# Weight preparation between the turns of attention in a four-layer transformer kernel

## Chip, cores and metric

The kernel runs on one core of a Trainium2 chip, as one program in fp32. The metric is device time in microseconds (us) of one execution; lower is better. Engines are named as in the profile: PE is the matmul engine (PEld its weight loads), DVE the vector engine, ACT the scalar engine, POOL the general one; SP issues most DMAs.

## What is computed

Four layers, each of them a half-weighted feed-forward, an attention and the same feed-forward again, on 1024 tokens (4 sequences of 256) of width 256, every block on the layer-normed x and added to x:

```
x = x + 0.5 * ffn0(norm(x));  x = x + attn0(norm(x));  x = x + 0.5 * ffn0(norm(x))
x = x + 0.5 * ffn1(norm(x));  x = x + attn1(norm(x));  x = x + 0.5 * ffn1(norm(x))
... the same for layers 2 and 3
```

What the change touches:

- attn0: 16 heads of 16. The scores are q.k to the power 4, causal, divided by their sum; no exponential.
- ffn0: silu(gate) * up, 688 hidden units. ffn1: 8 experts of 176 hidden units, the best 2 per token by a router, and a shared part of 352.
- attn1 works with a latent of 64 numbers per token, in the reference like this:

```
lat = rmsnorm(x @ wkv_a_w.T, norm_w);  k, v = split(lat @ wkv_b_w.T)
q = x @ wq_w.T + wq_b                    (16 heads of 128, half of each rotated by `freqs`)
o = softmax(mask(q k^T * scale)) v;      out = o @ out_w.T + out_b
```

  The rotation turns q and k of one head alike, so the kernel needs only the squared length of each pair of `freqs`, and it multiplies the weights of a head with each other: wq with the key half of wkv_b gives w.m (query weights that act on the latent directly), the value half of wkv_b with out_w gives w.n. This is "the merge".
- layer 2 needs its router, its shared expert's gate, up and down weights, and the taps and biases of three short convolutions, all transposed on PE before use ("the turns").

## The kernel before

**Tokens and order.** x lies in eight tiles of 128 tokens. `norm` (L164) takes the statistics per half (four tiles), a chain of small DVE instructions for the inverse root (`rsqrt`, L154), the normalized tile (L179), two PE transposes per tile (L135) and a copy into xT (by `copy`, L137, which alternates DVE and ACT). Every matmul goes through `mm` (L131), every addition to x through `add_to_x` (L203), so these lines stand for many groups in the profile; the tile names tell them apart: `mmb`, `trb` and `accb` are PSUM banks, `slot` a block of weights.

**Banks.** PSUM has eight banks. `banks(mm, tr, acc)` (L103) deals them out per stage. The feed-forwards have 4 for matmuls, 2 for transposes, 2 for sums. The two attentions have 0, 2, 2 and take the other four as two tiles of two banks each, named `s`, for scores (pool `l0s` in layer 0, `l1s` in layer 1).

**Layer-0 attention** (`l0_attn`, L339). Two kinds of generators: `tokens` makes q, k and v of 128 tokens, rotates and normalizes them and transposes them; `group` does four heads of one sequence: scores into two `s` tiles (16 rows per head), two squarings on ACT (L420, L421), the causal cut on POOL (L423), the sums over values into `accb` (L437, L439). The fourth group of a sequence also forms the denominators (L452), divides (L458) and multiplies by w.o. `staggered` (L473) drives them: in each turn every live generator makes one step, and one new generator may join, up to eight. There are 33 turns.

**Layer-1 attention** (`l1_attn`, L700) has 32 units (4 sequences by 8 pairs of heads) in the same manner, six at a time (L790): scores into an `s` tile, exponential on ACT (L755), division on POOL (L761), transposes through `trb`, context sums, and in the last unit of a sequence the multiplication by w.n.

**The merge** (`l1_attn_weights`, L606) is a generator of five steps. The first issues loads. The second does the prologue (squared lengths, two small transposes and those of w.a) and part 0, the others parts 1 to 3. Each part does four heads: `dk` on POOL (L665), eight transposes of out_w through `trb` with copies to `oT`, 16 matmul instructions into `mp`, 8 into `np_`, copies of both banks into the weight slot, 8 tiny matmuls for the bias, and it issues the next loads (`load`, L627, and `load_out`, L639; the buffer of `wo` is single). `mp` and `np_` (L668, L669) are two matmul banks.

**The turns.** `l2_ffn_weights` (L815) loads into a staging pool, transposes and copies: router, gate, up, down. The staging tile `b` of gate and up is single, so that up's load waits until gate has been transposed. `l2_attn_weights` (L1027) loads small tensors and transposes 15 blocks of 16 columns into one bank.

**Where they stand** (`program`, L1706): the first step of the merge before the first layer-0 feed-forward; parts 0 and 1 after layer-0 attention, before the second layer-0 feed-forward; parts 2 and 3 and both of layer 2's preparations after it, before the first layer-1 feed-forward.

The source order sets priorities only. The framework gives each engine a fixed order in which an instruction goes ahead of earlier ones when its operands and buffers are free sooner: the multiplication of L1041, which belongs to layer 2, runs at 69.42 us. The prologue and the first transposes of part 0 run from 248.54 on, in the attention's tail.

Of the kernel before, what the change touches and what calls it, by code (L numbers as in the profile page):

```python
# [2 lines left out]

# [6 lines left out]
F32 = mybir.dt.float32  # L10
# [8 lines left out]
P = 128  # L19
B, S, D = 4, 256, 256  # L20
# [202 lines left out]
def staggered(parts, width, apart):  # L223
    for _ in turns(parts, width, apart):
        pass
# [110 lines left out]
                m.add_to_x(t, o[:, :D], 0.5)  # L336


def l0_attn(m, w):  # L339

# [3 lines left out]
    nc, io = m.nc, m.io  # L344
    m.norm()
    with ExitStack() as ctx:
        pool = lambda name, bufs, **kw: ctx.enter_context(m.tc.tile_pool(name=name, bufs=bufs, **kw))
        one, wk, pairs = pool("l0a1", 1), pool("l0a", 2), pool("l0s", 2, space=PSUM)
# [116 lines left out]
        def parts():  # L465
            yield from (tokens(0, 0), tokens(0, 1))
            for b in range(B):
                for g in range(4):
                    yield group(b, g)
                    if b + 1 < B and g < 2:  # L470
                        yield tokens(b + 1, g)

        staggered(parts(), width=8, apart=1)  # L473

# [131 lines left out]
def l1_attn_weights(m, stage):  # L606
# [3 lines left out]
    nc, io = m.nc, m.io  # L610
# [35 lines left out]
    def trace():  # L646
        loads, o = [load(0), load(1)], load_out(0)
        yield
        nc.gpsimd.memset(len2[:, :64], scale)
        nc.vector.tensor_tensor(fr, fr, fr, ALU.mult)  # L650
        both = len2[:, 64:].rearrange("h (j r) -> h j r", r=2)
        for r in range(2):
            nc.vector.tensor_tensor(both[:, :, r], fr[:, :, 0], fr[:, :, 1], ALU.add)
        nc.vector.tensor_scalar(len2[:, 64:], len2[:, 64:], scale, None, ALU.mult)
        tb = m.tr_bank()
        m.tr(tb[:, :16], len2)
        m.tr(tb[:, 16:32], bq)
        for k in range(KC):
            m.tr(tb[:, 32 + k * 64 : 96 + k * 64], a[:, k * P : (k + 1) * P])
        nc.vector.tensor_copy(cols, tb[:, :32].rearrange("p (i h) -> p i h", i=2))  # L660
        nc.vector.tensor_copy(w.a, tb[:, 32:160].rearrange("p (k c) -> p k c", k=2))
        for g in range(4):
            q, kv = loads[g]
            dk = stage.tile([P, 4, 64], F32, name="dk", bufs=1)
            nc.gpsimd.tensor_tensor(  # L665
                dk, kv[:, 0], cols[:, 0, 4 * g : 4 * g + 4].unsqueeze(2).to_broadcast([P, 4, 64]), ALU.mult
            )
            mp = m.mm_bank().rearrange("p (k f) -> p k f", k=2)  # L668
            np_ = m.mm_bank().rearrange("p (f d) -> p f d", f=2)  # L669
            for i in range(4):  # L670
                if i % 2 == 0:
                    tb = m.tr_bank()
                    for j in range(2):
                        for k in range(KC):
                            m.tr(tb[:, (2 * j + k) * P : (2 * j + k + 1) * P], o[:, k, (i + j) * P : (i + j + 1) * P])
                    oT = stage.tile([P, 2, D], F32, name="oT", bufs=1)
                    m.copy(oT, tb.rearrange("p (j d) -> p j d", j=2))
                    for k in range(KC):
                        for j in range(2):
                            c = (i + j) * 64  # L680
                            m.mm(mp[:, k, c : c + 64], [(q[:, i + j, k * P : (k + 1) * P], dk[:, i + j, :])])
                    for j in range(2):
                        m.mm(np_[64 * j : 64 * j + 64, i // 2, :], [(kv[:, 1, i + j, :], oT[:, j, :])])
            m.copy(w.m[:, :, 256 * g : 256 * g + 256], mp)
            m.copy(w.n[:, 2 * g : 2 * g + 2, :], np_)
            bp = m.tr_bank()
            for i in range(4):
                out = bp[64 * (i % 2) : 64 * (i % 2) + 64, i // 2 : i // 2 + 1]
                m.mm(out, [(dk[:, i, :], cols[:, 1, 4 * g + i : 4 * g + i + 1])])
            nc.vector.tensor_copy(w.bg[:, 2 * g : 2 * g + 2], bp[:, :2])  # L690
            if g < 3:
                o = load_out(g + 1)
            if g < 2:
                loads.append(load(g + 2))
            yield
# [1 line left out]
    return w, trace()  # L697


def l1_attn(m, w):  # L700

    nc = m.nc
    m.norm()
    with ExitStack() as ctx:
# [82 lines left out]
                    m.mm(o[:, :D], [(ctxT[b][:, f, i * P : (i + 1) * P], w.n[:, f, :]) for f in range(8)])  # L787
                    m.add_to_x(2 * b + i, o[:, :D], 1.0)

        staggered((unit(b, p) for b in range(B) for p in range(8)), width=6, apart=1)  # L790

# [20 lines left out]
    return got  # L812


def l2_ffn_weights(m):  # L815
    nc, io = m.nc, m.io
    w = SimpleNamespace()
    w.r = m.small.tile([P, KC, 64], F32, name="l2_router")
    w.sg = m.small.tile([P, KC, 192], F32, name="l2_sg")
    w.su = m.small.tile([P, KC, 192], F32, name="l2_su")  # L820
    w.sd = m.small.tile([96, 2, D], F32, name="l2_sd")
    with m.tc.tile_pool(name="l2w", bufs=1) as wk:
        a = wk.tile([64, D], F32, name="a")
        nc.sync.dma_start(out=a, in_=io.L2_ffn_gate_w)
        tb = m.tr_bank()
        for k in range(KC):
            m.tr(tb[:, k * 64 : k * 64 + 64], a[:, k * P : (k + 1) * P])
        m.copy(w.r, tb[:, :128].rearrange("p (k e) -> p k e", k=KC))
        for src, out in ((io.L2_ffn_shared_gate_w, w.sg), (io.L2_ffn_shared_up_w, w.su)):
            a = wk.tile([96, 2, D], F32, name="b")  # L830
            nc.sync.dma_start(out=a, in_=src.rearrange("(f p) d -> p f d", p=96))
# [5 lines left out]
        a = wk.tile([P, 2, 192], F32, name="c")  # L837
        nc.sync.dma_start(out=a, in_=io.L2_ffn_shared_down_w.rearrange("(c p) f -> p c f", p=P))
        tb = m.tr_bank()
        for f in range(2):  # L840
            for c in range(2):
                m.tr(tb[:96, f * D + c * P : f * D + (c + 1) * P], a[:, c, f * 96 : f * 96 + 96])
        m.copy(w.sd, tb[:96, : 2 * D].rearrange("p (f d) -> p f d", f=2))
    return w


def l2_ffn(m, w, tables, tail=None):
# [176 lines left out]
                m.add_to_x(t, got[:, k], 0.5)  # L1024


def l2_attn_weights(m):  # L1027
# [15 lines left out]
    with m.tc.tile_pool(name="l2aw", bufs=1) as wk:  # L1043
        tb = m.tr_bank()
        for i, n in enumerate("qkv"):
            taps = wk.tile([16, P, 4], F32, name=f"taps{i}")
            nc.sync.dma_start(out=taps, in_=getattr(io, f"L2_attn_{n}cw").rearrange("(h p) j -> h p j", h=16))
            bias = wk.tile([16, P], F32, name=f"bias{i}")
            nc.sync.dma_start(out=bias, in_=getattr(io, f"L2_attn_{n}cb").rearrange("(h p) -> h p", h=16))
            for j in range(5):  # L1050
                at = (i * 5 + j) * 16
                m.tr(tb[:, at : at + 16], taps[:, :, j] if j < 4 else bias)
        m.copy(w.conv, tb[:, :240].rearrange("p (i j h) -> p i j h", i=3, j=5))
    return w


def l2_attn(m, w):
# [648 lines left out]
def program(tc, io):  # L1706
    with ExitStack() as ctx:
# [4 lines left out]
        with tc.tile_pool(name="small2", bufs=1) as small2:  # L1712
            with slots() as m.wts:
                with tc.tile_pool(name="small1", bufs=1) as m.small:
                    with tc.tile_pool(name="l1w", bufs=2) as stage:
# [73 lines left out]
```

## Time and profile before

| | us |
|---|---|
| median of 9 runs | 2119.18 (2101.92 to 2124.5) |
| the profiled execution, its own time | 2119.13 |
| its span in the profile | 2117.4 |
| PE busy in the span | 1827.4 |
| mean granted PE clock | 0.907 of full speed |

The page cuts the span into 40 slices of 53 us, with a digit for the busy share of each engine in each slice; a digit of `PEclk` is the granted clock in tenths. A table by stretches gives for chosen windows the busy time and the number of instructions of each engine, then the clock, the DMA share and the traffic. In the timeline a line is a run of like instructions of one engine; a bracket tells the idle time ahead of it and who ended that. Matmul ends are modelled, and a slow clock makes the same matmul look longer, so a busy PE is not PE at full speed.

The stages around the change, from PE's timeline: first layer-0 feed-forward to 113.2 us, layer-0 attention from 121.7 to 259.9, second layer-0 feed-forward to 337.2, first layer-1 feed-forward to 514.5, layer-1 attention to 698.9, second layer-1 feed-forward after that.

### The profile page before, as it was taken

To read this page: it belongs to the slowest core of one execution; us is meant where nothing else is said; L and a number is where in the kernel's file an instruction comes from. 1 tells how busy PE (TensorE), PEld (TensorE's weight loads), DVE (VectorE), ACT (ScalarE), POOL (GpSimd) and SP (SyncE) were. 2 spreads that over 40 slices of the span, in tenths; PEclk is the share of its full clock that TensorE was granted. 3 is DMA by queue.
4 is the path that set the end of the run, shared out by engine and by line. 5 is a ranking of instruction groups with operands and counts; after the bars stand their busy time and mean duration, and the time that the engine had idled before them with its cause. 6 is when DMAs were issued, how large, how long until landed. Compare 5 with 4: busy or idle time off the path is not lost. (4 is left out here: it accounts for less than half of the span.)

```text
span 2117.4 us, 33750 instructions
## 1 busy us (share of the span) xinstructions
PE 1827.4 (86%) x12924; PEld 1191.5 (56%) x12924; DVE 1201.8 (57%) x2918; ACT 700.3 (33%) x1565; POOL 572.7 (27%) x1125
## 2 busy tenths in 40 slices
PE   3978998999899999487659999999999955889889
PEld 2444655466566566353336677667777743446556
DVE  8654433333555433545778887787775654463571
ACT  7336411211545201121324554544545521101210
POOL 0024200000333000176334425434323215730210
PEclk9978798999899999698779999999999987968889
DMA  8000013226000213295120111111011049730000
GB/s 229 3 0 1 11 40 85 74 67 217 1 1 1 76 45 80 84 295 191 48 81 22 42 41 51 34 49 41 12 37 41 11 120 259 237 130 0 5 0 20
DMA packets 121872, 147.38 MB, mean 70 GB/s; under 512 B 18008, under 2 KB 95472, under 8 KB 121712
## 3 DMA queue, kind: packets, MB, share of 16 engines
q1 hardware_dynamic: 115568, 126.34, 20.0%
q0 software_dynamic: 6144, 18.88, 2.8%
q8 instruction: 103, 1.69, 0.3%
q14 instruction: 57, 0.47, 0.1%
HBM read 120.03 MB, written 25.17 MB: 69 GB/s over the span
## 5 line engine op out<-in xcount | busy, mean ns | idle before, releaser
L131 PE MATMUL mmb<-xT,slot 128*128 128x512 f32 (+2 forms) x768 | 347.0, 608 | 3.0 <-DVE h L197 1.0
L131 PEld LDWEIGHTS mmb<-xT,slot 128*128 128x128 f32 (+2 forms) x768 | 143.3, 190 | 181.2 <-issue 173.3
L131 PE MATMUL accb<-slot,h 128*128 128x256 f32 (+1 forms) x896 | 201.2, 382 | 0.0
L131 PEld LDWEIGHTS accb<-slot,h 128*128 128x128 f32 (+1 forms) x896 | 167.5, 190 | 37.0 <-issue 15.8
L203 DVE SCALAR_TENSOR_TENSOR x<-accb,x 128x256 f32<-128x256 f32 x112 | 47.1, 421 | 206.0 <-PE accb L131 205.8
L1148 DVE SCALAR_TENSOR_TENSOR qT<-mmb,l_conv,qT 128x510 f32<-128x510 f32 (+2 forms) x96 | 70.8, 738 | 57.8 <-ACT qT L1144 56.8
L579 ACT ACTIVATE sg<-mmb 128x512 f32<-128x512 f32 (+1 forms) x56 | 33.4, 597 | 196.4 <-PE mmb L131 196.4
L1148 DVE SCALAR_TENSOR_TENSOR vT<-mmb,l_conv,vT 128x510 f32<-128x510 f32 (+2 forms) x96 | 71.1, 740 | 18.1 <-ACT vT L1144 17.2
L761 POOL TENSOR_TENSOR e<-e,den 128x512 f32<-128x512 f32 x64 | 51.5, 826 | 105.4 <-DVE den L758 105.4
L948 POOL DMA_INDIRECT rows<-table,source x64 | 61.9, 968 | 58.7 <-issue 28.3
L996 POOL DMA_INDIRECT parts<-os,target x64 | 66.3, 1036 | 21.9 <-issue 13.3
L1194 POOL TENSOR_TENSOR put<-lt,t_same 32x128 f32<-32x128 f32 x128 | 63.9, 499 | 27.4 <-DVE lt L1189 20.6
L977 DVE SCALAR_TENSOR_TENSOR h<-sg,rows,mmb 64x96 f32<-64x96 f32 x128 | 40.1, 313 | 51.9 <-ACT sg L972 49.8
L581 DVE TENSOR_TENSOR sg<-sg,c 128x512 f32<-128x512 f32 x44 | 30.8, 701 | 67.0 <-ACT sg L579 32.9
L131 PE MATMUL accb<-wo,zT 128*128 128x256 f32 x256 | 63.0, 400 | 6.1 <-DVE x L203 4.5
L1148 DVE SCALAR_TENSOR_TENSOR kT<-mmb,l_conv,kT 128x510 f32<-128x510 f32 (+2 forms) x96 | 66.3, 736 | 2.2 <-ACT kT L1144 2.0
L143 ACT COPY xT<-trb 128x256 f32<-128x256 f32 x44 | 16.3, 371 | 153.0 <-PE trb L135 143.7
L967 PE MATMUL mmb<-slot,gx 128*64 128x192 f32 x512 | 62.1, 366 | 5.2 <-DVE gx L141 5.2
L131 PE MATMUL mmb<-xT,wq 128*128 128x512 f32 x128 | 66.5, 643 | 0.0
L131 PE MATMUL mmb<-xT,wv 128*128 128x512 f32 x128 | 63.5, 618 | 0.0
L131 PE MATMUL mmb<-xT,wg 128*128 128x512 f32 x128 | 60.8, 596 | 0.0
L131 PEld LDWEIGHTS accb<-wo,zT 128*128 128x128 f32 x256 | 50.5, 201 | 18.0 <-DVE x L203 5.7
(445 smaller groups left out, 4074.0 us busy)
## 6 DMA issues: line engine op xcount, KB each, us to landing
slot<-_L_ffn_gate_up_proj_dram SPq DMA_DIRECT2D x16, 1536.0 KB, 19.6
slot<-in_L_ffn_down_proj_dram SPq DMA_DIRECT2D x8, 1536.0 KB, 20.3
parts<-zero SPq DMA_DIRECT2D x16, 768.0 KB, 9.8
got<-parts SPq DMA_DIRECT2D x16, 768.0 KB, 4.4
bca<-scr SPq DMA_DIRECT2D x32, 256.0 KB, 3.3
bcb<-scr SPq DMA_DIRECT2D x32, 256.0 KB, 3.1
c<-rows SPq DMA_DIRECT2D x16, 256.0 KB, 3.2
table<-xs SPq DMA_DIRECT2D x2, 1280.0 KB, 5.0
```

The costliest lines, as they stand in the source:

```text
L131: self.nc.tensor.matmul(out=out, lhsT=a, rhs=b, start=i == 0, stop=i == last, **kw)
L143: self.nc.scalar.copy(out, in_)
L203: self.nc.vector.scalar_tensor_tensor(self.x[t], got, scale, self.x[t], ALU.mult, ALU.add)
L579: nc.scalar.activation(sg[:n], g[:n], AF.Silu)
L581: nc.vector.tensor_tensor(sg, sg, c, ALU.mult)
L761: nc.gpsimd.tensor_tensor(e[:, :, cut], e[:, :, cut], den[:, i, :].unsqueeze(2).to_broadcast([P, 2, n]), ALU.mult)
L948: nc.gpsimd.indirect_dma_start(out=r, out_offset=None, in_=table, in_offset=bass.IndirectOffsetOnAxis(ap=slot[0][:, 2 * g + i : 2 * g + i ...
L967: nc.tensor.matmul(out=ps[half, i, :], lhsT=xT[:, i, k, half], rhs=gu[:, 4 * (g % 2) + 2 * i + j, k, :], start=k == 0, stop=k == KC - 1,)
L977: nc.vector.scalar_tensor_tensor(h[half, i, :], sg[half, i, :], rows[i][half, D + e : D + e + 1], ps[half, i, 96:], ALU.mult, ALU.mult,)
L996: ins = nc.gpsimd.indirect_dma_start(out=parts, out_offset=bass.IndirectOffsetOnAxis(ap=slot[1][:, 2 * g + i : 2 * g + i + 1], axis=0), in ...
L1148: nc.vector.scalar_tensor_tensor(yi[:, :, d:], ps[:, :, : S - d], tap(j), yi[:, :, d:], ALU.mult, ALU.add)
L1194: nc.gpsimd.tensor_tensor(batches[b].put[rows(q), :, :, u * G : u * G + G], lt[rows(q), :, rows(q)].rearrange("p c (z t) -> p t z c", z=2) ...
```

## The change

The merge's parts are no longer run at the two borders around layer-0's second feed-forward. `l0_attn` gets the generator and calls its next step after every seventh turn; what is left is run behind the last turn. Within a part, `mp` and `np_` are the two banks of one `s` tile instead of two matmul banks. Both of layer 2's preparations are split: the loads are issued right after layer-0 attention, into a pool of their own that lives until layer-1 attention ends (gate and up now have a staging tile each); the transposes and copies are a generator that `l1_attn` steps after every fourth turn, in three steps: router, gate and up; down; taps and biases.

```diff
-def l0_attn(m, w):
+def l0_attn(m, w, between):
...
-        staggered(parts(), width=8, apart=1)
+        m.two_banks = lambda: pairs.tile([P, 2, 512], F32, name="s")
+        for i, _ in enumerate(turns(parts(), 8, 1)):
+            if i % 7 == 6:
+                next(between, None)
+        for _ in between:
+            pass
...
-            mp = m.mm_bank().rearrange("p (k f) -> p k f", k=2)
-            np_ = m.mm_bank().rearrange("p (f d) -> p f d", f=2)
+            both = m.two_banks()
+            mp, np_ = both[:, 0].rearrange("p (k f) -> p k f", k=2), both[:, 1].rearrange("p (f d) -> p f d", f=2)
...
-def l1_attn(m, w):
+def l1_attn(m, w, between):
...
-        staggered((unit(b, p) for b in range(B) for p in range(8)), width=6, apart=1)
+        for i, _ in enumerate(turns((unit(b, p) for b in range(B) for p in range(8)), 6, 1)):
+            if i % 4 == 3:
+                next(between, None)
+        for _ in between:
+            pass
...
-def l2_ffn_weights(m):
+def l2_ffn_weights(m, wk):
...
+    r = wk.tile([64, D], F32, name="a")
+    nc.sync.dma_start(out=r, in_=io.L2_ffn_gate_w)
+    shared = []
+    for name, out in (("gate", w.sg), ("up", w.su)):
+        a = wk.tile([96, 2, D], F32, name=f"b_{name}")
+        nc.sync.dma_start(out=a, in_=getattr(io, f"L2_ffn_shared_{name}_w").rearrange("(f p) d -> p f d", p=96))
+        shared.append((a, out))
+    down = wk.tile([P, 2, 192], F32, name="c")
+    nc.sync.dma_start(out=down, in_=io.L2_ffn_shared_down_w.rearrange("(c p) f -> p c f", p=P))
+
+    def trace():
         tb = m.tr_bank()
...
+        yield
+
+    return w, trace()
...
                         with m.banks(0, 2, 2):
-                            l0_attn(m, w0)
+                            l0_attn(m, w0, parts)
+                    with tc.tile_pool(name="l2w", bufs=1) as stage:
+                        m.small = small2
+                        (w2, turned), (wb, more) = l2_ffn_weights(m, stage), l2_attn_weights(m, stage)
                         with m.banks(4, 2, 2):
-                            next(parts), next(parts)
                             l0_ffn(m, w0)
-                            next(parts), next(parts)
-                            m.small = small2
-                            w2, wb = l2_ffn_weights(m), l2_attn_weights(m)
                             l1_ffn(m, w1)
-                    with m.banks(0, 2, 2):
-                        tables = l2_tables(m)
-                        l1_attn(m, wa)
+                        with m.banks(0, 2, 2):
+                            tables = l2_tables(m)
+                            l1_attn(m, wa, chain(turned, more))
```

`turns` (L206) is the loop that `staggered` ran before; it yields after each turn. `l2_attn_weights` is split like `l2_ffn_weights`.

More of the change, by code (lines that the diff above doesn't have):

```diff
@@ L1 @@
 from contextlib import ExitStack, contextmanager, nullcontext
+from itertools import chain
 from types import SimpleNamespace
@@ L821, in l2_ffn_weights @@
     w.sd = m.small.tile([96, 2, D], F32, name="l2_sd")
-    with m.tc.tile_pool(name="l2w", bufs=1) as wk:
-        a = wk.tile([64, D], F32, name="a")
-        nc.sync.dma_start(out=a, in_=io.L2_ffn_gate_w)
+    r = wk.tile([64, D], F32, name="a")
[8 more added lines that the diff above has]
+    def trace():
         tb = m.tr_bank()
         for k in range(KC):
-            m.tr(tb[:, k * 64 : k * 64 + 64], a[:, k * P : (k + 1) * P])
+            m.tr(tb[:, k * 64 : k * 64 + 64], r[:, k * P : (k + 1) * P])
         m.copy(w.r, tb[:, :128].rearrange("p (k e) -> p k e", k=KC))
-        for src, out in ((io.L2_ffn_shared_gate_w, w.sg), (io.L2_ffn_shared_up_w, w.su)):
-            a = wk.tile([96, 2, D], F32, name="b")
-            nc.sync.dma_start(out=a, in_=src.rearrange("(f p) d -> p f d", p=96))
+        for a, out in shared:
             tb = m.tr_bank()
@@ L836, in l2_ffn_weights @@
             m.copy(out, tb[:, :384].rearrange("p (k f) -> p k f", k=KC))
-        a = wk.tile([P, 2, 192], F32, name="c")
-        nc.sync.dma_start(out=a, in_=io.L2_ffn_shared_down_w.rearrange("(c p) f -> p c f", p=P))
+        yield
         tb = m.tr_bank()
@@ L841, in l2_ffn_weights @@
             for c in range(2):
-                m.tr(tb[:96, f * D + c * P : f * D + (c + 1) * P], a[:, c, f * 96 : f * 96 + 96])
+                m.tr(tb[:96, f * D + c * P : f * D + (c + 1) * P], down[:, c, f * 96 : f * 96 + 96])
         m.copy(w.sd, tb[:96, : 2 * D].rearrange("p (f d) -> p f d", f=2))
-    return w
+        yield
+    return w, trace()
 def l2_ffn(m, w, tables, tail=None):
@@ L1024, in l2_ffn, with l2_attn_weights @@
                 m.add_to_x(t, got[:, k], 0.5)
-def l2_attn_weights(m):
+def l2_attn_weights(m, wk):
     nc, io = m.nc, m.io
@@ L1042, in l2_attn_weights, with trace @@
     w.conv = m.small.tile([P, 3, 5, 16], F32, name="l2_conv")
-    with m.tc.tile_pool(name="l2aw", bufs=1) as wk:
-        tb = m.tr_bank()
[L1045 to L1049, printed above, removed]
+    taps = []
+    for i, n in enumerate("qkv"):
+        t, bias = wk.tile([16, P, 4], F32, name=f"taps{i}"), wk.tile([16, P], F32, name=f"bias{i}")
+        nc.sync.dma_start(out=t, in_=getattr(io, f"L2_attn_{n}cw").rearrange("(h p) j -> h p j", h=16))
+        nc.sync.dma_start(out=bias, in_=getattr(io, f"L2_attn_{n}cb").rearrange("(h p) -> h p", h=16))
+        taps.append([t[:, :, j] for j in range(4)] + [bias])
+    def trace():
+        tb = m.tr_bank()
+        for i in range(3):
             for j in range(5):
                 at = (i * 5 + j) * 16
-                m.tr(tb[:, at : at + 16], taps[:, :, j] if j < 4 else bias)
+                m.tr(tb[:, at : at + 16], taps[i][j])
         m.copy(w.conv, tb[:, :240].rearrange("p (i j h) -> p i j h", i=3, j=5))
-    return w
+        yield
+    return w, trace()
 def l2_attn(m, w):
```

## The prediction

> **What bounds the kernel now.** I read the slices of the page first, then busy time by stretches, then PE's timeline at the stage borders. The page says that PE is busiest and that its clock dips in slices 3 to 5 (layer-0 attention), 7 and 13.
>
> ```profile
> PE 1827.4 (86%) x12924; PEld 1191.5 (56%) x12924; DVE 1201.8 (57%) x2918; ACT 700.3 (33%) x1565; POOL 572.7 (27%) x1125
> ...
> PEclk9978798999899999698779999999999987968889
> ```
>
> The table by stretches has: start and end, length, then busy us (and instructions) of PE, PEld, DVE, ACT, POOL, then the granted clock. The stretches are layer-0 attention; the border behind it, to the steady matmuls of the feed-forward; the border between the second layer-0 and the first layer-1 feed-forward, in two pieces; layer-1 attention; and the start of the second layer-1 feed-forward.
>
> ```profile
> 121.70:259.90 138.20, 119.96 (x790) 72.43 (x791) 61.27 (x118) 72.75 (x122) 48.73 (x89) 0.76 0.02 5
> 259.90:273.30 13.40, 11.93 (x85) 7.84 (x84) 8.75 (x32) 3.79 (x8) 1.22 (x2) 1.00 0.54 158
> ...
> 337.20:357.40 20.20, 13.26 (x100) 9.91 (x99) 7.22 (x26) 3.40 (x6) 0.98 (x2) 0.75 0.58 141
> 357.40:380.30 22.90, 22.65 (x93) 14.74 (x92) 9.95 (x49) 6.33 (x11) 0.00 (x0) 0.77 0.01 3
> 514.50:698.90 184.40, 161.20 (x961) 108.26 (x959) 102.93 (x252) 88.37 (x331) 57.66 (x71) 0.93 0.00 1
> 698.90:718.60 19.70, 19.18 (x78) 10.79 (x78) 11.26 (x62) 7.17 (x11) 0.00 (x0) 0.91 0.27 80
> ```
>
> Both attentions are PE with small holes (18.2 us of idle in 138.2, 23.2 in 184.4); layer-0 attention runs at 0.76 of the clock. Between 337.2 and 357.4 PE does only weight preparation, at 66%. Its timeline there (start, duration, operation, and in brackets the idle time and who ended it):
>
> ```profile
> 337.20 0.66 PE L135 MATMUL trb<-t_ident,wo 128*128 128x128 f32 x4
> ...
> 345.47 1.07 PE L135 MATMUL trb<-t_ident,wo 128*128 128x128 f32 x8 [1.57 <-DMA wo<-in_L_attn_out_w_dram]
> ...
> 353.26 0.87 PE L135 MATMUL trb<-t_ident,b 96*128 96x96 f32 x4 [2.54 <-DMA b<-n_L_ffn_shared_up_w_dram]
> ...
> 356.82 0.63 PE L135 MATMUL trb<-t_ident,taps 16*128 16x16 f32 x4 [1.83 <-DMA taps<-in_L_attn_qcw_dram]
> ...
> 365.45 2.05 PE L131 MATMUL mmb<-xT,slot 128*128 128x512 f32 x2
> ```
>
> Layer 1's first feature matmul comes 28 us after the last layer-0 matmul, with three waits on loads that had just been issued.
>
> **What is removed.** Border B, 337.2 to 380.3 (end of the share transposes), is 43.1 us. It holds parts 2 and 3 of the merge, layer 2's turns, 5.9 us of load waits, and the norm that is queued behind them. The nearest row for what stays is the second layer-1 feed-forward: 19.7 us from the last attention matmul to the same transposes. It did 28 feature matmuls in that time, not 24 (less 4 x 0.44 = 1.8), and had turned its first half of x already (plus 8 x 0.165 = 1.3). Without parts ahead of it, half 0 waits for transposes and copies: where layer-1 attention follows a feed-forward, 514.5 to the first 512-wide matmul at 517.97 is 3.5; part of it is router work, so 2.5. 19.7 - 1.8 + 1.3 + 2.5 = 21.7: **21.4 us go** (18 to 24). Next late there is DVE's chain for half 1 (337.3 to about 342), under half 0's matmuls.
>
> Border A, 259.9 to the end of the gate and up matmuls at 292.4, is 32.5. What stays: 48 matmuls x 0.436 = 20.9, half 1's transposes 1.4, and a wait for the last addition to x to free a bank, 0.5 as at 699.43 (22.8; half 0's transposes can move into the attention's tail). **About 9 go** (7 to 10). Sum of both: 30.4.
>
> **What is added to layer-0 attention.** One part is 8 transposes of wo (1.25), 16 dk,wq matmul instructions (2.2), 8 oT,wkv (1.3) and 8 of the bias (0.5): 5.2 us at full clock, from the rows at 259.8 to 268. Four parts and 0.7 for the prologue are 21.5, of which about 2.5 (prologue and first transposes, 248.5 to 252.2) lie in this stretch already: 19 us are new for PE. DVE and ACT get 2.7 per part for copies and POOL 0.6; all three are under 55% busy. Walking the generators, the parts come behind turns 6, 13, 20 and 27 of 33: between the first group's scores and the second's (about 149 us in this trace), behind batch 1's last scores (181), in batch 2's tail (220), and ahead of batch 3's sums (247).
>
> What 19 us of PE cost is the open term. The clock is half in busy slices, too (4 us each):
>
> ```profile
> 152.00:156.00 4.00, 4.00 (x36) 2.69 (x30) 1.52 (x3) 3.75 (x7) 1.66 (x6) 0.50 0.00 0
> 156.00:160.00 4.00, 4.00 (x42) 2.77 (x36) 0.00 (x0) 3.68 (x6) 2.26 (x5) 0.50 0.00 0
> ...
> 208.00:212.00 4.00, 1.44 (x18) 0.65 (x10) 2.82 (x4) 2.69 (x6) 2.31 (x5) 0.85 0.00 2
> ```
>
> At 152 to 160 PE is full and cold: a part there takes double. At 208 to 212 it is idle 2.6 us, and then cold till about 221. Lower bound: the parts fill the holes and keep the clock at layer-1 attention's 0.93; PE's work at full clock is 120.0 x 0.76 + 19 = 110, and 110 / 0.93 / 0.90 busy = 132, 6 us less than today. Upper bound: all of it cold and in line, 19 / 0.5 = 38, plus the 4.6 us for which a part holds a score tile (259.8 to the copy at 264.4): +43. I take the clock of the better stretch 196 to 220, 0.81, and PE at 90%: 110 / 0.81 / 0.90 = 151, **+13**, and +1 for the score tile.
>
> The score tile: a part takes one of the two double-bank tiles that every group of four heads needs both of. Only part 0 meets a group that is waiting: ACT (1.55 us per tile, 93% busy from 148 to 160) runs from one tile meanwhile. Parts 1 to 3 fall where no scores are due.
>
> [...]
>
> **What is added to layer-1 attention.** Layer 2's turns: 0.5 + 0.9 + 0.9 + 1.1 (rows at 348.4 to 355) and the 15 small ones of the taps, 2.8: 6.1 us of PE and 2.3 of copies, behind turns 3, 7 and 11, about 545 to 565. 23.2 us of holes lie in the stage, but 546 to 570 is nearly full. Between 0 and 6.1 / 0.5 = 12; I take **+4**, the turns less a third that fits holes. They also use the two transpose banks of the units, one to three us each.
>
> **At nothing:** the loads. Each part issues the next part's load of wo (5.9 us to landing, seven turns ahead) on SP; layer 2's small loads move ahead of layer-0's second feed-forward, to wait for the merge's staging memory. SP's next own work is the expert slots at 325 and 339, needed much later; were the loads in the way, the 20 us landing of those still has layer 1 as cover. One odd number of copies changes places, so the DVE/ACT alternation flips: 0.1 us a copy.
>
> **Sum** against the profiled execution, 2119.1 (span 2117.4; the median of the runs shown is 2119.2): -21.4 - 9 + 14 + 4 = -12.4: **2107 us**.
>
> **Rivals.** (1) Absorbed: the parts warm the clock and fill holes, payback 0 to 12: 2089 to 2101. For it: at the rate of the fast rows (scores of a group 0.94, its weighted values 1.06, 512-wide 0.455) layer-0 attention's matmuls would need some 86 us, 62% of its span; against: the cold full slices. (2) Paid back: PE is the bound there, 24 to 40: 2113 to 2129. (3) Slower: the parts, cold and in line, hold a score tile and the transpose banks while groups and tokens wait. Its price is 43 + 12 less 30 = up to +25; it decides from 41 us of payback (layer-0 attention over about 170 us long): 2130 to 2144. (4) It doesn't do what it says: instructions keep no source order here (a layer-2 multiplication, L1041, ran at 69.4), so the parts can slide to the attention's end and border A stays: 2112 to 2119.
>
> **How the numbers follow.** Forecast (payback 12 to 24, 2101 to 2113): 0.40, two thirds of it under 2108.6. (1) 0.22, (2) 0.15, (3) 0.18, (4) 0.05. Half a per cent, 10.6 us, is about what a measurement of this kernel can tell from no change. Faster 0.27 + 0.22 = 0.49; same 0.13 + 0.15 + 0.05 = 0.33; slower 0.18. The unknown terms span 2079 to 2149; 2090 to 2134 leaves out under 2 in 10. The forecast's own range is 2101 to 2113. The nine runs lie at 2102 to 2104 (three) and 2117 to 2125 (six), so a median may sit 16 us off for that alone.
>
> **What would show it.** Border B under 24 us with no wait on wo, b or taps; the first gate matmul within 1 us of the last attention matmul; layer-0 attention at 150 to 154 us with a clock near 0.8; layer-1 attention at 186 to 190. I am wrong if layer-0 attention is over 165, or not longer at all, or if dk matmuls stand after its last addition to x.

## The result, and the profile after

The changed kernel is slower: a ratio of 1.012 to the kernel before (95% interval 1.0097 to 1.0144; medians of 2138.6 and 2108.2 us over 20 and 62 runs). Its profiled execution took 2135.7 us (span 2134.0), 16.6 more than that of before. 2107 was forecast, with 2134 as the end of the range.

The page of the changed kernel: PE's busy time is up by 2.6 us only, in a span that is 16.6 longer. The clock digits differ in the fourth and fifth slices (layer-0 attention), the seventh (border B), the tenth and eleventh (the start of layer-1 attention) and four later ones.

```profile
PE 1830.0 (86%) x12924; PEld 1192.3 (56%) x12924; DVE 1200.8 (56%) x2918; ACT 700.4 (33%) x1565; POOL 573.8 (27%) x1125
...
PEclk9976899998799999788678999999999987968889
```

The same stages as in the prediction, by stretches (start and end, length, busy us and instructions of PE, PEld, DVE, ACT, POOL, clock, DMA share, GB/s): layer-0 attention, the border behind it, the border before layer 1's first feed-forward, layer-1 attention.

```profile
121.60:281.20 159.60, 142.29 (x940) 89.08 (x940) 67.95 (x132) 78.00 (x131) 50.61 (x92) 0.76 0.09 26
281.20:304.10 22.90, 22.31 (x58) 9.10 (x56) 8.90 (x29) 5.87 (x10) 0.00 (x0) 1.00 0.00 1
348.90:368.50 19.60, 18.91 (x86) 10.94 (x86) 12.76 (x67) 6.58 (x11) 0.00 (x0) 1.00 0.40 81
500.90:718.60 217.70, 167.67 (x991) 112.24 (x989) 104.40 (x256) 89.69 (x333) 58.20 (x72) 0.88 0.19 61
```

| stretch | before | after | difference | forecast |
|---|---|---|---|---|
| layer-0 attention | 138.2 | 159.6 | +21.4 | +14 |
| border A | 32.5 | 22.9 | -9.6 | -9 |
| border B | 43.1 | 19.6 | -23.5 | -21.4 |
| layer 1's first feed-forward behind it | 134.2 | 132.4 | -1.8 | 0 |
| layer-1 attention | 184.4 | 217.7 | +33.3 | +4 |
| all the rest, to the end | | | -3 | 0 |

Until layer-1 attention begins the changed kernel is 13.5 us ahead. There it loses 33. The last columns of its line have the hint: a stretch that moved next to nothing before (0.00, 1 GB/s) now has a DMA share of 0.19. PE's timeline at its start:

```profile
515.19 1.98 PE L132 MATMUL accb<-xT,slot 128*128 128x512 f32 x4 [0.78 <-ACT query L745]
547.30 1.97 PE L136 MATMUL trb<-t_ident,lat 128*128 128x128 f32 x8 [30.13 <-POOL lat L730]
```

In the kernel before the same place has a wait of 3.0 us:

```profile
532.59 1.97 PE L135 MATMUL trb<-t_ident,lat 128*128 128x128 f32 x8 [3.01 <-POOL lat L724]
```

So PE now stands idle for 30.1 us. It waits for `lat`, and `lat` for `raw`, the first tile of the stage, which DVE copies out of PSUM. DVE's timeline says what that copy waited for, in the kernel before and then in the changed one:

```profile
526.22 0.69 DVE L714 COPY raw<-accb 128x512 f32<-128x512 f32 x1 [1.78 <-PE accb L131]
```

```profile
541.50 0.69 DVE L720 COPY raw<-accb 128x512 f32<-128x512 f32 x1 [31.76 <-DMA parts<-zero]
```

In the changed kernel it is a transfer that has nothing to do with layer-1 attention. `l2_tables` fills a small tile, `zero` (1280 bytes per partition), with zeros, and 18 DMAs write it over tables in DRAM that layer 2 needs 350 us later. POOL and SP's queue, first in the kernel before, then after:

```profile
350.10 0.36 POOL L801 MEMSET zero<- 128x320 f32 x1 [8.25 <-PE mmb L131]
```

```profile
469.98 0.38 SPq L805 DMA_DIRECT2D table<-zero  x1
470.42 13.34 SPq L807 DMA_DIRECT2D parts<-zero  x8
483.80 2.12 SPq L805 DMA_DIRECT2D table<-zero  x1
485.97 17.61 SPq L807 DMA_DIRECT2D parts<-zero  x8
510.17 0.34 SPq L99 DMA_DIRECT2D t_causal<-in_consts_dram  x1
```

```profile
501.25 0.36 POOL L811 MEMSET zero<- 128x320 f32 x1 [51.16 <-PE accb L132]
```

```profile
501.64 0.34 SPq L815 DMA_DIRECT2D table<-zero  x1
502.03 13.51 SPq L817 DMA_DIRECT2D parts<-zero  x8
515.59 1.85 SPq L815 DMA_DIRECT2D table<-zero  x1
517.49 16.30 SPq L817 DMA_DIRECT2D parts<-zero  x8
541.21 0.34 SPq L100 DMA_DIRECT2D t_causal<-in_consts_dram  x1
```

The fill has moved from 350 to 501, and the transfers with it, from 470 to 501.6; they last until 541. The kernel before orders them in the same way, and its `raw` waits for them as well: in the compiled programs of both, five waits on all eight DMA counters stand in front of that copy. They were over at 510.2, and `raw` could be copied at 526.2, so that wait had ended before the one for the matmuls, and showed nowhere. Now they are over 31.0 later and the stage is 13.4 earlier: 31.0 + 13.4 - 16.0 of slack is 28.4, and that is about the loss.

### The profile page after: what moved, and what is told of

It reads as the page before. It is cut to its first block, busy times and chain, and to the rows that moved or that the text cites. A ratio compares the mean times of both kernels' runs of the same rounds, so it can differ in the third digit from the quotient of the medians.

```text
span 2134.0 us, 33728 instructions
## 1 busy us (share of the span) xinstructions
PE 1830.0 (86%) x12924; PEld 1192.3 (56%) x12924; DVE 1200.8 (56%) x2918; ACT 700.4 (33%) x1565; POOL 573.8 (27%) x1125
## 5 line engine op out<-in xcount | busy, mean ns | idle before, releaser
L966 POOL DMA_INDIRECT rows<-table,source x64 | 61.9, 968 | 57.5 <-issue 30.1
L1218 POOL TENSOR_TENSOR put<-lt,t_same 32x128 f32<-32x128 f32 x128 | 63.9, 499 | 27.3 <-DVE lt L1213 20.5
L132 PE MATMUL mmb<-xT,wk 128*128 128x512 f32 x128 | 60.9, 627 | 0.0
```

Of the source, the lines that this page charges most:

```text
L132: self.nc.tensor.matmul(out=out, lhsT=a, rhs=b, start=i == 0, stop=i == last, **kw)
L966: nc.gpsimd.indirect_dma_start(out=r, out_offset=None, in_=table, in_offset=bass.IndirectOffsetOnAxis(ap=slot[0][:, 2 * g + i : 2 * g + i ...
L1218: nc.gpsimd.tensor_tensor(batches[b].put[rows(q), :, :, u * G : u * G + G], lt[rows(q), :, rows(q)].rearrange("p c (z t) -> p t z c", z=2) ...
```

## The experiments

**The theories.** Theory 1, memory: the new staging pool stays open until layer-1 attention ends, so the pool of `zero`, opened above it, no longer lies in memory of the merge (free since 350) but in memory in which layer 1's feed-forward has just worked. The compiled addresses agree: `zero` lies at 143040 in the kernel before, where the merge's `fr` lay, and at 157376 in the changed one, 14336 bytes further, which is the size of the staging pool; there lay a tile `shareT0` of layer 1's feed-forward. So the fill waits for the feed-forward, and the pools of layer-1 attention, which open on the same place when the pool of `zero` is closed, wait for the transfers. Both waits are for a whole pool and not for the bytes that overlap: the DMAs that read `shareT` are issued at 369 us, but the fill waits until the feed-forward's last matmul at 501, and `raw` begins at 158912, behind the end of `zero` at 158656. Theory 2: the parts in layer-0 attention are the loss (the prediction's slower case). Theory 3: the transfers disturb the stage that they run beside, by traffic or by the queue that they fill.

The table has all kernels, read at the same events of PE: from the first q, k, v matmul of layer-0 attention to the first gate matmul of the feed-forward behind it (F); border B; from the first query matmul of layer-1 attention to the transposes of `lat` (H); from its first scores to layer 1's second router (U); and the time of that router. The ratio is to the kernel before.

| kernel | F | B | H | U | router at | ratio (95%) |
|---|---|---|---|---|---|---|
| before | 148.7 | 42.2 | 14.6 | 164.9 | 699.4 | 1 |
| changed | 160.3 | 18.6 | 42.8 | 169.9 | 719.1 | 1.0120 (1.0097 to 1.0144) |
| zero_staged | 161.3 | 18.6 | 13.3 | 169.4 | 690.5 | 0.9959 (0.9929 to 0.9990) |
| zero_late_kept | 160.4 | 18.6 | 13.3 | 167.0 | 686.2 | 0.9947 (0.9915 to 0.9978) |
| before_zero_late | 149.2 | 44.6 | 43.1 | 162.5 | 728.7 | 1.0178 (1.0131 to 1.0225) |
| merge_only | 161.1 | 40.0 | 14.6 | 164.9 | 710.4 | 1.0036 (1.0003 to 1.0069) |
| turns_at_border | 160.5 | 25.2 | 14.6 | 165.7 | 694.7 | 0.9998 (0.9965 to 1.0032) |
| first_early | 148.6 | 22.0 | 13.3 | 173.5 | 684.6 | 0.9936 (0.9902 to 0.9970) |
| early_tail | 154.5 | 20.3 | 13.3 | 172.1 | 689.6 | 0.9974 (0.9943 to 1.0005) |
| all_behind | 162.9 | 20.3 | 13.3 | 172.2 | 696.9 | 0.9978 (0.9944 to 1.0012) |
| both_gaps | 154.7 | 18.6 | 13.3 | 164.8 | 679.7 | 0.9928 (0.9902 to 0.9954) |
| turns_first | 146.4 | 18.6 | 13.3 | 168.7 | 673.8 | 0.9909 (0.9876 to 0.9942) |

(B here runs from the last layer-0 matmul to the first share transpose, some 1 us less than the 43.1 and 19.6 above.)

**1. zero_staged: the changed kernel with the zero tile in the staging pool.**

```diff
-def l2_tables(m):
+def l2_tables(m, wk):
...
-    with m.tc.tile_pool(name="zeros", bufs=1) as wk, m.tc.issue_after(m.spread.ins):
+    with m.tc.issue_after(m.spread.ins):
...
-                            tables = l2_tables(m)
+                            tables = l2_tables(m, stage)
```

> The changed kernel with one edit: the zero tile of layer 2's tables is allocated in the staging pool that stays open, not in a pool of its own above it. Theory 1 (memory): the fill of the tile waits for layer 1's feed-forward only because it lies in that feed-forward's memory, and raw (the first tile of layer-1 attention) waits for the transfers that read it; so the fill moves to before 360 us, the 18 zero transfers are issued from about 456 instead of 501.6, the hole of 30.1 us ahead of the lat transposes goes, layer-1 attention takes 186 to 190 instead of 217.6, and the whole 2105 in its own execution, a ratio of about 0.993 to the kernel before. Theory 2 (the parts in layer-0 attention are the loss): layer-1 attention may change but the total stays within 5 us of the changed kernel's 2135. Theory 3 (the transfers cost by themselves, wherever they lie): the 30 us turn up where the transfers now are, 456 to 505.

The fill went to 274.6, the transfers are issued from 458.3 to 490.8, and the hole is gone. PE, DVE:

```profile
519.71 1.09 PE L136 MATMUL trb<-t_ident,lat 128*128 128x128 f32 x8 [1.75 <-POOL lat L730]
```

```profile
513.92 0.69 DVE L720 COPY raw<-accb 128x512 f32<-128x512 f32 x1 [2.34 <-PE accb L132]
```

`raw` now waits for its matmuls (2.34 us) and PE 1.75. Layer-1 attention takes 187.5, inside the 186 to 190. Three lines of code turn a loss of 1.2% into a gain of 0.4%. Theory 2 falls: layer-0 attention is as long as in the changed kernel, and the total is below that of before. So does theory 3 as it was put here, since nothing turned up at 458 to 491.

**2. zero_late_kept: the fill and the transfers stay late, but their memory is not taken.**

```diff
-    with m.tc.tile_pool(name="zeros", bufs=1) as wk, m.tc.issue_after(m.spread.ins):
+    with m.tc.issue_after(m.spread.ins):
...
-                        with m.banks(0, 2, 2):
-                            tables = l2_tables(m)
+                        with m.banks(0, 2, 2), tc.tile_pool(name="zeros", bufs=1) as zeros:
+                            tables = l2_tables(m, zeros)
```

> The changed kernel with the zero tile as late as there (it lies in memory of layer 1's feed-forward, so it is filled at about 501), but its pool stays open beside layer-1 attention's tiles, so that none of these takes its memory. Theory 1, memory alone: raw waits for nothing but its matmuls, and the whole hole of 30.1 us goes; about 2105. Theory 1 with the queue: raw, lat and the first queries go on, but t_causal is issued on SP behind the 18 zero transfers (at about 534, landing at 540 to 545), the first units wait for it at the causal addition, and a hole of 15 to 22 us stays, now on t_causal; about 2122 to 2127. Theory 3 (the transfers themselves slow the engines): the stage stays at 217.

SP's queue and the line of the hole:

```profile
501.13 0.35 SPq L100 DMA_DIRECT2D t_causal<-in_consts_dram  x1
501.56 0.40 SPq L815 DMA_DIRECT2D table<-zero  x1
502.01 13.57 SPq L817 DMA_DIRECT2D parts<-zero  x8
515.62 1.87 SPq L815 DMA_DIRECT2D table<-zero  x1
517.54 17.45 SPq L817 DMA_DIRECT2D parts<-zero  x8
```

```profile
517.79 1.09 PE L136 MATMUL trb<-t_ident,lat 128*128 128x128 f32 x8 [1.75 <-POOL lat L730]
```

The transfers are issued at the same times as in the changed kernel, to 0.1 us, and the hole is gone as fully as in the first experiment; the stage takes 185.1 with a DMA share of 0.22 in it. This is memory alone. The variant with the queue missed: once `t_causal` needs no memory of `zero`, the framework issues it ahead of the transfers, so its place behind them in the changed kernel came from the same reuse. Theory 3 is out in both forms.

**3. before_zero_late: the kernel before, only with the memory of `zero` made late.**

```diff
                             w2, wb = l2_ffn_weights(m), l2_attn_weights(m)
-                            l1_ffn(m, w1)
+                    with m.banks(4, 2, 2):
+                        l1_ffn(m, w1)
```

> The kernel before with nothing of the change, but layer 1's first feed-forward runs after the pool of the staging tiles is closed, so its tiles lie at the bottom of that memory, where the zero tile comes next. Theory 1: the fill of the zero tile moves from 350 to about 515 (behind the feed-forward), the transfers from 470 to about 516, raw waits for them, and a hole of 28 to 31 us opens at the start of layer-1 attention: 2148 in its own execution, 1.013 to 1.015 of the kernel before. If the hole of the changed kernel came from something else in the change (the turns between units, the order of the small loads), it does not open here: within 3 us of the kernel before.

Nothing is moved but the closing of a pool. POOL, DVE, PE:

```profile
518.05 0.36 POOL L801 MEMSET zero<- 128x320 f32 x1 [51.16 <-PE accb L131]
```

```profile
558.52 0.69 DVE L714 COPY raw<-accb 128x512 f32<-128x512 f32 x1 [30.81 <-DMA parts<-zero]
```

```profile
564.32 1.97 PE L135 MATMUL trb<-t_ident,lat 128*128 128x128 f32 x8 [31.25 <-POOL lat L724]
```

The same hole, 31.3 us, opens in the kernel before (28.5 more in H), and it costs 1.8% (1.3 to 2.3), a little above the 1.3 to 1.5 expected; at the second router the kernel is 29.3 us late. The turns and the small loads have no part in it.

**4. merge_only: the merge's parts between the turns of layer-0 attention, layer 2 prepared at border B as before.** `l2_ffn_weights` and `l2_attn_weights` are those of the kernel before; a pool that nothing uses holds the merge's memory, so that `zero` is free early.

```diff
-                    with tc.tile_pool(name="l2w", bufs=1) as stage:
+                    with tc.tile_pool(name="l1w", bufs=2) as stage:
+                        stage.tile([P, 2752], F32, name="held")
                         with m.banks(4, 2, 2):
                             l0_ffn(m, w0)
+                            m.small = small2
+                            w2, wb = l2_ffn_weights(m), l2_attn_weights(m)
                             l1_ffn(m, w1)
```

> The merge alone: its parts lie between the turns of layer-0 attention as in the changed kernel, layer 2's small weights are prepared at the border before layer 1's first feed-forward as in the kernel before, and the zero tile lies in memory that is free early. By the sum of the measured terms: layer-0 attention +21.4 (159.6), the border behind it -9.6 (22.9), the border before layer 1's feed-forward less two parts of the merge, some 12 to 14 of its 43.1, with the waits on b and taps still there, layer-1 attention 184 with no hole. Total -1 (2117 to 2120), a ratio of 0.998 to 1.002. If the parts are what makes the changed kernel slow, it is slower by 15 or more here too.

There is no hole, as expected, but the kernel is 0.4% slower than before and not level (the interval begins just above 1, and at the second router the profile is 11.0 us late): border B gave back 2.2 us and not 12 to 14. PE's timeline there:

```profile
352.73 0.31 PE L136 MATMUL trb<-t_ident,a 64*128 64x64 f32 x2 [2.31 <-DMA a<-in_L_ffn_gate_w_dram]
354.09 0.55 PE L136 MATMUL trb<-t_ident,b 96*128 96x96 f32 x4 [1.05 <-DMA b<-L_ffn_shared_gate_w_dram]
363.91 0.87 PE L136 MATMUL trb<-t_ident,b 96*128 96x96 f32 x4 [9.27 <-DMA b<-n_L_ffn_shared_up_w_dram]
```

Parts 2 and 3 had covered layer 2's loads. Without them PE waits 14.6 us for loads (with 1.92 for `taps`) where it waited 5.9 before. The load of `up` is issued behind the transpose of `gate`, whose staging tile it takes, at 354.7, and by then the 1.5 MB (1536 KB) of an expert slot are ahead of it (issued at 352.2); PE waits 9.27 us for it, 2.54 in the kernel before. What the prediction says of border B holds only for both moves together.

**5. turns_at_border: zero_staged, with layer 2's turns back at border B, but their loads early.**

```diff
                             l0_ffn(m, w0)
+                            for _ in chain(turned, more):
+                                pass
                             l1_ffn(m, w1)
...
-                            l1_attn(m, wa, chain(turned, more))
+                            l1_attn(m, wa, iter(()))
```

> The kernel with the zero tile in the staging pool, but layer 2's turns back at the border ahead of layer 1's feed-forward, with their loads issued early as in the changed kernel. If what the border lost by the change is mostly waits on those loads, it grows from 19.6 to 25 to 28 us (the turns alone are 6.1 of PE), with no wait on a, b, c or taps, and layer-1 attention gets 1 to 4 shorter: total 2 to 6 more than the kernel with the staged zero tile. If it is the place of the turns that counts, the border goes back to about 41, as with the merge alone, and the total is 15 to 20 more.

B is 25.2, 14.8 us less than with the merge alone, with no wait for a load in it, for the same turns in the same place: the gain of that half of the change is mostly the earlier loads. At the second router the kernel is 4.2 us behind zero_staged, inside the 2 to 6 that were expected; by the ratios it is 0.0039 of 2107, some 8 us, but the intervals overlap.

**6. first_early: zero_staged, with the first part of the merge behind turn 3.**

```diff
-            if i % 7 == 6:
+            if i in (3, 13, 20, 27):
```

> The kernel with the zero tile in the staging pool, and the first part of the merge moved from behind turn 6 to behind turn 3 of layer-0 attention: ahead of the first pad transposes, where PE waits 4.7 us (132 to 137) and then runs 137 to 141 at 0.50. Theory 1 (a part costs what its place makes of it: in a busy cold place 9.5 us, in a gap little): the first part costs 0 to 4 instead of 9.5, and the first second-half matmuls of layer 0's feed-forward come 6 to 9 us earlier (at 308 to 311 instead of 316 to 318); total about 7 less than the kernel with the staged zero tile. Theory 2 (5.2 us of PE per part is paid wherever it lies, since PE is the bound): no change within 2 us.

F falls by 12.7, more than the 6 to 9 expected, and theory 2 (5.2 us wherever the part lies) falls. Counted at the sums of the first sequence's denominators, a part further on, the first part costs 3.1 us where it cost 10.2 in zero_staged, which is the term that was expected. The other 5.5 came with the second part, which did not move. PE's timeline at it, in zero_staged and then here:

```profile
188.74 0.62 PE L438 MATMUL accb<-p,v 128*32 128x256 f32 x2
192.23 1.97 PE L132 MATMUL s<-dk,wq 128*128 128x64 f32 x8 [2.88 <-ACT p L421]
...
195.19 1.97 PE L132 MATMUL s<-dk,wq 128*128 128x64 f32 x8
```

```profile
180.81 0.62 PE L438 MATMUL accb<-p,v 128*32 128x256 f32 x2
184.31 1.10 PE L132 MATMUL s<-dk,wq 128*128 128x64 f32 x8 [2.88 <-ACT p L421]
...
185.93 1.33 PE L132 MATMUL s<-dk,wq 128*128 128x64 f32 x8
```

The same instructions behind the same wait of 2.88 us (the part wants an `s` tile that ACT still reads, a cost that the prediction gave to the first part alone) run cold in one kernel, 1.97 us for eight matmuls (clock 0.50 from 191.7), and warm in the other, 1.10 (1.0 until 186.7).

**7. early_tail: as 6, with only the first and one other part between turns, two at the end** (`if i in (3, 27)`).

> As the kernel with the first part early, and the other three moved too: one behind turn 27 (ahead of the last sums), two behind the last turn, at the border to the feed-forward. Theory 1: the second and third part no longer lie in stretches at 0.50 (they cost 6.8 and 4.9 there); behind the last turn they run at full clock, partly in the waits of the attention's tail, as two did in the kernel before (9.6 for two). Layer 0's second-half matmuls at 306 to 310, 2 us either way of the kernel with only the first part early. Theory 2: 316 to 318 as before. If parts between turns are hidden work, as the change intends, it is slower than the kernel with only the first part early by 5 or more.

F is 154.5, 5.9 more than in first_early and 6.8 less than in zero_staged. Theory 1 had it within 2 of first_early, so this missed; the last sentence of the expectation fits better. But experiments 9 and 10 give F values 8 us apart for one code, so whether the later parts are cheaper between the turns or at the end stays open.

**8. all_behind: zero_staged with all four parts behind the last turn** (`if i in ()`).

> The kernel with the zero tile in the staging pool, and all four parts behind the last turn of layer-0 attention, one after the other, as the kernel before had two of them there. If laying parts between the turns hides any of their work, this is slower than the kernel with the staged zero tile by 5 to 12 us. If the four parts cost their PE time at full clock in either place (21 in a row, 21.4 measured between the turns), it is the same within 3: second-half matmuls of layer 0's feed-forward at 314 to 319.

162.9 against 161.3, and ratios that overlap. So the profiles show 1.6 us hidden by laying the parts between the turns as the change does, and not the 5 to 12 of the first branch (at the second router it is 6.4 us behind zero_staged, but most of that arose behind F, in stages that the edit does not touch). This is one profile of all_behind, and the ratios alone do not rule out 5 us: that the change's layer-0 half pays nearly as much as the parts in a row would is likely, not shown.

**9. both_gaps: as 6, with layer 2's turns behind turns 1, 2 and 3 of layer-1 attention** (`if i in (1, 2, 3)` for `if i % 4 == 3`).

> The kernel with the staged zero tile and the first part early, and layer 2's turns moved from behind turns 3, 7 and 11 of layer-1 attention to behind turns 1, 2 and 3: between the first scores and the third query's, where PE waits 4.3 us for the first exponentials. Six kernels with the turns at 3, 7 and 11 have 167 to 173.5 from the first scores to the second router of layer 1; three without turns there have 162.5 to 165.7. If a step costs what its place makes of it, 163 to 168 here, and a total 3 to 6 less than the kernel with the first part early. If the 6.1 us of PE are paid wherever they lie, or the turns hold up the copies that the first units need, 169 or more and no gain. Layer-0 attention has the same instructions as in the kernel with the first part early: if the cold stretches belong to the kernel and not to the run, its first gate matmul comes again 148 to 149.5 behind its first qkv matmul.

U is 164.8; without any turns it was 162.5 to 165.7 in four kernels, and with the turns at 3, 7 and 11 it was 167.0 to 173.5 in six. PE's wait for the first exponentials, in first_early and then here:

```profile
517.70 1.19 PE L132 MATMUL s<-latT,query 64*128 64x256 f32 x2 [3.67 <-ACT e L761]
```

```profile
519.99 1.64 PE L132 MATMUL s<-latT,query 64*128 64x256 f32 x6 [1.49 <-ACT e L761]
```

The wait is filled in part, and the turns cost nothing that shows. How much of the 2 to 9 us is the place and how much the clock is open, since the same turns in the same place gave values 6.5 us apart. The guess on the clock missed: F is 154.7 with the same layer-0 attention that gave 148.6. For the total see below the next one.

**10. turns_first: the same turns behind turns 0, 1 and 2** (`if i < 3`).

> As the kernel with both steps in gaps, but layer 2's turns behind turns 0, 1 and 2, so that they stand ahead of most of the first unit's scores on PE instead of behind them. Then they delay the first scores and with them the first exponentials by their 3 to 6 us, and the wait for these (4.3 us) stays: from the transposes of lat to the second router 2 to 5 more than with turns 1, 2 and 3. If only the sum of PE's work counts, the same within 1.

From the transposes of `lat` to the second router it takes 170.3, both_gaps 166.2: 4.1 more, within the 2 to 5. The first scores then come behind the turns, and the gap stays open after them. F, on the other hand, is 146.4, again another value for the same code. On the chip that ran 9 and 10 the kernel before took 2157.9 in the median, and the expert matmuls of layer 2's first feed-forward (`mmb<-slot,gx`, first to last) take 88 and 90 us in the two profiles where they take 66 to 69 in the ten others, so their spans are not set beside those of the others, only their ratios and the stages up to the second router. By the ratios first_early, both_gaps and turns_first (0.994, 0.993, 0.991) can't be told apart; each is faster than the kernel before. The kernels with the two steps in gaps are 20 and 26 us ahead of before at the second router.

## Why the prediction was wrong

**The step that failed** is the one put as "**At nothing:** the loads", for the staging pool. It asked what the early loads wait for, and what is queued behind them on SP, both rightly costed at nothing. It did not ask what the pool's longer life takes from the tiles that come after it: the pool moved `zero` up by 14 KB into the feed-forward's memory. The profile of before shows all that was needed: the fill at 350.1, the transfers from 470 to 510 directly ahead of layer-1 attention, and `raw` at 526. That is a slack of 16 us, against transfers of 40 us that now start 31.7 later. Experiments 1 to 3 take this cause away in two ways and put it into the kernel before; it is shown. It costs 28.1 us in H (42.75 against 14.62). With it taken away the changed kernel stands 8.9 (zero_staged) and 13.2 us (zero_late_kept) ahead of before at the second router, where the prediction's sum had 12.4.

**Border B**: right in size (-23.5 for -21.4). The reason given was half of it: experiments 4 and 5 show that the early loads carry it, and that without them 14.6 us of waits take the place of the parts.

**Border A**: right (-9.6 for -9); the first gate matmul comes 0.7 us behind the last one of the attention, within 1 was forecast.

**Layer-0 attention**: mis-sized, +21.4 for +14, within its bounds of -6 to +43. 19 us of work at 0.81 of the clock were assumed; it ran at 0.76 as before. The four parts cost 9.5, 6.7, 5.2 and 2.3 us (shifts of like events against before; 23.7 in all, of which some 2.3 lay in the stretch of before already, as the prediction said). The row at 152 to 160 was read rightly, a part there takes double, and then averaged away. The wait for a score tile was given to the first part alone; the second waits 2.88 us for one as well (experiment 6).

**The turns in layer-1 attention**: +5.0 in U for +4, on the stated rows; in the place of experiment 9 U is level with before.

**Copies**: "0.1 us a copy" was too little, though the rows of before have it (a copy into `oT` takes 0.69 us on DVE, 0.59 on ACT). The feed-forward of layer 1 (from the first share transpose to the first `l_a` matmul) takes 134.4 in all eight kernels with the turns behind it and 136.0 in all four with them ahead, and H without a hole 13.3 and 14.6. The swap of DVE and ACT in the order of the copies is the likely reason; it wasn't tried by itself.

**The rivals**: the slower case came true in sign, for none of its reasons. Its point of decision, layer-0 attention over about 170 us, was not reached (159.6). Nor did any of the three signs of being wrong appear: layer-0 attention was longer, but not over 165, and no `dk` matmul stands behind its last addition to x. What did tell was layer-1 attention, 217.7 where 186 to 190 was stated. (One slip on which nothing rests: the digit of the page that dips in layer-1 attention is the eleventh, not the thirteenth.)

## What to carry to other kernels

A pool that lives longer moves every pool that is opened above it: list the tiles that come next, see whose memory they get now, and which waits in the profile of before have only a little slack (here 16 us, for 40 us of transfers) and so show nowhere. Work put between other work is worth what the place makes of it: look for a place where the engine waits (132 to 137 and the first exponentials here), not for an even spacing. A load wait that does not show may be covered by the very work that a change takes away.

## What the runs showed of the hardware

The granted clock of PE is 1.0 or 0.50 in the clock records of the kernel before and of the changed one (68 and 60 records), and each stretch at one value, but for the last of each, is a whole multiple of 3.41 us long. In the kernel before it is 0.50 from 118.61 to 125.43 (6.8 us), 1.0 to 135.67 (10.2), 0.50 to 142.50 (6.8). In layer-0 attention of that kernel it drops seven times: three times in a wait of PE (of 4.72, 2.27 and 1.95 us, at 135.7, 180.1 and 210.8), four times where the timeline has no wait (at 149.3, 231.3, 238.1 and 251.7). The time until it comes back differs much for the same instructions: at the wait of 2.88 us it is 0.50 from 191.7 to 212.2 in zero_staged, 20.5 us, with PE busy at 100% from 196 to 212; in first_early it stays at 1.0 through that wait until 186.7 and is 0.50 for 6.8. Four profiles with the same layer-0 attention as the changed kernel give F within 1 us of it; three with the first part early give 148.6, 154.7 and 146.4. Transposes ran at either clock: eight of `wo` take 1.09 us at 187.7 in zero_staged (clock 1.0), eight of `pad` 1.97 at 137.1 in the kernel before (0.50). What keeps PE cold while it is busy stays open.

Layer 3's first feed-forward with the weight preparation ahead of it, far behind the change, takes 109 to 112 us in some profiles and 93 to 99 in others. The mean clock in it is 0.78, 0.78 and 0.79 in before, changed and both_gaps (111.4, 111.4 and 110.6 us), and 0.93 and 0.89 in zero_staged and zero_late_kept (95.2 and 99.4). In the kernel before PE is busy at 100% from 1881.5 to 1915.7, and the clock is 0.50 all that time. The long form is in before, changed, before_zero_late, merge_only and all_behind, among others, the short one in zero_staged, zero_late_kept and first_early, among others. That is why spans of single executions are not compared above. The runs of before lie in two groups about 16 us apart, the same size; that it is this stage was not tried.

The 12.9 MB of zeros move at 323 GB/s (mean from 501 to 541 in the changed kernel, DMA share 0.98), and beside layer-1 attention they slow nothing that can be seen (experiment 2: U is 167.0 with them and 169.4 in zero_staged without).
